# Step 2 of a sparse-attention graph layer: one block's sum moved in front of the mask, gathers issued one by one, a rearranged end

## The chip, the cores and the metric

The kernel runs on one core of one Trainium2 chip. The core has five engines that work at the same time, each through its own queue in order: the tensor engine (PE), the vector engine (DVE), the scalar engine (ACT), GpSimd (POOL), and SP, which here only issues DMA. The metric is device microseconds of one launch. The kernel before took 1431.23 us (median of 3 runs, 1426.26 to 1432.77).

## The reference

There are 3327 nodes with 256 features. `h = relu(layernorm(x))` goes through two diffusion steps along two paths:

```
Xf = R @ Xf                 # R: adjacency plus identity, rows divided by their sum (sparse: 0.12% filled)
A  = top-p attention of Xa  # softmax of q k^T, in each row only the largest entries that
                            # together reach 0.9 of the mass, divided by their sum
Xa = A @ Xa
Z  = Z + Xf @ U1[n].T + Xa @ U2[n].T      # n = 0, 1
out = x + layernorm(h + Z)
```

The attention is dense before it is cut: 3327 x 3327 exponentials per step, and a threshold per row. The threshold is what makes the kernel long; a row must be looked at several times until it is exact.

## The kernel before

Rows are worked on in 26 tiles of 128. For every tile the kernel does this:

- **weights** (L580): PE makes a row tile of logits in four pieces (`pl`, L598), ACT takes their exponential into `e`, 128 x 3328 (L602, L606).
- **measured** (`measured_twice` in step 2, L666): ACT passes three times over `e` and counts (`ja`, L631 in `through`), with short arithmetic of one value per row between the passes, on ACT, DVE and POOL. Out comes a guess that lies just above the threshold. POOL's part is L674 and L675, L687 to L689, and L694 to L709; the last of it, L709, feeds ACT's L711.
- **settle** (L722): DVE zeroes all that is above the guess and sums (L728), takes the largest 8 of every 168-wide segment (20 MAX8, L733), sorts some 48 candidates out of them (L740, L742), finds the exact threshold, and cuts `e` with it (L762, which this document calls the mask; L759, in two parts, for the first and last tile).
- **Sums** (L798): the cut `e` is transposed on PE block by block (`turn`, L811, 4 transposes of 128 x 128 into one of two PSUM banks `pt`), ACT copies each block to SBUF (`eT`, L813, three buffers), and PE multiplies it with the features (`sum`, L825, into the one PSUM bank `pa`). A tile has seven blocks, 0 to 6; block 6 is half as long.
- **spread**, **diffuse** (L1073, L908): the path of R. Five rows of the adjacency and of the features per node were gathered in step 1 by indirect DMA on POOL's queue; in step 2 the packed adjacency rows are loaded again by SP (L1094) and the features are gathered again (`fetched`, L899, five gathers of L903 per tile), and PE multiplies (`pr`, L911).
- **finish** (L934), only in step 2: DVE adds the two paths (L935, which frees `pa`), then comes the layer norm: DVE L457 and L458, POOL L464, L465, L943, ACT L950, POOL L945, L951 and L952, and the output.

No scheduler orders this. Each of these functions is a Python generator that emits a few instructions and then yields. The main loop (L1116) runs for every step over `i` = -1 to 27; in round `i` tile `i` is settled, tile `i+1` is measured, and the tile before is summed. A round has seven parts, `k` = 0 to 6, and the strings in `PLAN` (L1103) name by letter which generator goes on in which part: m measured, n the measured of the round before, d settle, c the settle of the round before, s spread, w weights, q their beginning, l the laws, g the gathers, f finish. `LAST` (L1106) replaces them for the last rounds. Whatever is left at the end of a round runs there (L1175). PE, ACT, DVE and, from step 2 on, POOL keep exactly this order of text (L1183), so an instruction that waits holds up everything written behind it on its engine.

In step 2 each part first transposes the block that lies two ahead of the one to be summed (L1160; `AHEAD`), then runs the letters, then sums one block (L1166). With `LATE[1] = 4` the parts 0 to 3 of round `i` sum blocks 3 to 6 of tile `i-2`, and parts 4 to 6 blocks 0 to 2 of tile `i-1`. The mask of tile `i-1` (letter c) is emitted in part 0 of round `i`, and the transpose of its block 0 in part 2, where the sum of block 5 of the tile before comes behind it.

`laws` (L548) computes for the tiles 3 to 25 the constants that `measured_twice` takes; its last piece is POOL arithmetic over 128 x 23 values (L567 to L574), emitted at the end of round -1 of step 2. `refetch(t)` (L1092) issues the load and all five gathers of a tile at once; round -1 issues those of tiles 0 and 1, round `i` those of tile `i+2`.

Of the kernel before, what the change touches and what calls it, by code (L numbers as in the profile page):

```python
# [9 lines left out]
F32 = mybir.dt.float32  # L10
# [3 lines left out]
AF = mybir.ActivationFunctionType  # L14
ALU = mybir.AluOpType
# [3 lines left out]
P = 128  # L19
N = 3327  # L20
D = 256
DA = 64
NT = (N + P - 1) // P
# [315 lines left out]
KT = DIRECT + 2  # L339
# [5 lines left out]
def guess_graph_layer(ctx, tc, x, adj, w1t, w2t, w3t, u1t, u2t, ln_g, ln_b, out, flag):  # L345
    nc = tc.nc

    const = ctx.enter_context(tc.tile_pool(name="const", bufs=1))
    nodes = ctx.enter_context(tc.tile_pool(name="nodes", bufs=1))
    scan = ctx.enter_context(tc.tile_pool(name="scan", bufs=1))  # L350
    adjp = ctx.enter_context(tc.tile_pool(name="adjp", bufs=3))
# [9 lines left out]
    V, G, S, PE = nc.vector, nc.gpsimd, nc.scalar, nc.tensor  # L361

    rows_of = lambda t: min(P, N - t * P)
    valid = lambda t: 0 <= t < NT
# [41 lines left out]
    half = const.tile([P, 4], F32, tag="half", name="half")  # L406
    for k, c in enumerate((-0.5, 0.5, -1.0, -0.5)):
        G.memset(half[:, k : k + 1], c)
    halves = const.tile([P, NT], F32, tag="halves", name="halves")
    G.memset(halves, 0.5)  # L410
    law = const.tile([P, 7, NT], F32, tag="law", name="law")
    one = const.tile([P, 7], F32, tag="one", name="one")
    for k, c in enumerate((1.0, -1.0, 5.0e-4, SQG[1], SQK[1], math.log(10.0), LNY)):
        G.memset(one[:, k : k + 1], c)
    of_s = const.tile([P, 4], F32, tag="of_s", name="of_s")
    for k, c in enumerate((SQG[0], SQG[2], -SQK[0], -SQK[2])):
# [24 lines left out]
    bx = dram.tile([P, NT, D + 1], F32, tag="bx", name="bx")  # L441
    vx = dram.tile([P, NT, D], F32, tag="vx", name="vx")
# [4 lines left out]
    bb = const.tile([P, TOPK + 1], F32, tag="bb", name="bb")  # L447
# [100 lines left out]
    def laws(ts):  # L548

        at = lambda k, a, b: law[:, k, a:b]  # L550
        few_of = [ts[h::2][n : n + 3] for n in range(0, len(ts), 3) for h in range(2)]
        for few in filter(len, few_of):
            pq = ps_t.tile([P, 4, P], F32, tag="pt", name="pq")
            pm = pq.rearrange("p a b -> p (a b)")[:, : 3 * (2 * DA + 2)].rearrange("p (t n) -> p t n", t=3)
            for k, t in enumerate(few):
                PE.matmul(pm[:, k, :], query_of(t), qm[query_at(t), 1, :], start=True, stop=True)
            wide = scan.tile([P, NP], F32, tag="w", name="wide")
            mq = wide[:, : 3 * (2 * DA + 2)].rearrange("p (t n) -> p t n", t=3)
            V.tensor_copy(mq[:, : len(few)], pm[:, : len(few)])
            V.tensor_copy(law[:, 2, few[0] : few[-1] + 1 : 2], mq[:, : len(few), DA])  # L560
            for k, t in enumerate(few):
                V.scalar_tensor_tensor(mq[:, k, : DA + 1], mq[:, k, : DA + 1], 1.0, mq[:, k, DA + 1 :],
                                       ALU.mult, ALU.mult, accum_out=at(1, t, t + 1))
            yield
        a, b = ts[0], ts[-1] + 1
        s, var, m = (at(k, a, b) for k in range(3))
        G.tensor_tensor(s, var, halves[:, a:b], ALU.pow)  # L567
        for k, c in ((3, SQG[0]), (4, SQG[2]), (5, -SQK[0]), (6, -SQK[2])):
            G.tensor_scalar(at(k, a, b), s, c, 1.0e-4, ALU.mult, ALU.add)
        G.tensor_tensor(at(4, a, b), at(4, a, b), var, ALU.add)  # L570
        G.tensor_tensor(at(4, a, b), at(4, a, b), m, ALU.add)
        G.tensor_scalar(m, m, 0.25, LNY - 0.25 * math.log(0.1 / N), ALU.mult, ALU.add)
        G.tensor_scalar(var, var, 0.125, None, ALU.mult)
        G.tensor_tensor(var, var, m, ALU.add)  # L574
# [51 lines left out]
    def con(k):  # L626
        return one[:, k : k + 1]
# [247 lines left out]
    def gathered(t):  # L875
        oh = ohs.pop(t)
        ls, n = lists[:, t, :], LIST - DIRECT
        po = ps_t.tile([P, 4, P], F32, tag="pt", name="po")
        PE.matmul(po[:, 0, : n + 1], oh, ls[:, DIRECT:], start=True, stop=True)
        lo = small.tile([P, n], F32, tag="lo", name="lo", bufs=2)  # L880
        S.copy(lo, po[:, 0, :n])
        nth = small.tile([P, 1], F32, tag="nth", name="nth")
        S.activation(nth, po[:, 0, n : n + 1], AF.Identity, scale=-1.0, bias=part)
        yield
        of = small.tile([P, LIST], F32, tag="of", name="of", bufs=2)
        V.scalar_tensor_tensor(of[:, :n], place[:, :n], nth, lo, ALU.is_equal, ALU.mult, accum_out=nth)
        G.tensor_scalar(index[:, t, DIRECT:], nth, -1.0, float(NONE), ALU.mult, ALU.add)
        ac = adjp.tile([P, KT, P], F32, tag="ac", name="ac", bufs=2)
        nc.sync.dma_start(ac[:, KT - 1, :], adj[t, :, t, :])
        acs[t] = ac  # L890
        G.tensor_tensor(ac[:, KT - 1, :], ac[:, KT - 1, :], ident, ALU.add)
        rows = adj.rearrange("t p j r -> (t p j) r")
        for k in range(KT - 1):
            G.indirect_dma_start(out=ac[:, k, :], out_offset=None, in_=rows,  # L894
                                 in_offset=bass.IndirectOffsetOnAxis(ap=index[:, t, k : k + 1], axis=0),
                                 element_offset=t * P * NT * P)
        xgs[t] = fetched(bx, t, D + 1)

    def fetched(table, t, w):  # L899
        xg = adjp.tile([P, KT - 1, D + 1], F32, tag="xg", name="xg", bufs=2)  # L900
        rows = table.rearrange("p j d -> (p j) d")
        for k in range(KT - 1):
            G.indirect_dma_start(out=xg[:, k, :w], out_offset=None, in_=rows,  # L903
                                 in_offset=bass.IndirectOffsetOnAxis(ap=index[:, t, k : k + 1], axis=0))
        return xg


    def diffuse(ac, xg, own, w):  # L908
# [94 lines left out]
    for q in range(HALF + 5):  # L1003
        if 0 <= q - 3 < HALF:
            k, pk = q - 3, made.pop(q - 3)
# [17 lines left out]
        if 0 <= q - 2 < HALF:  # L1023
            k, pt = q - 2, turned.pop(q - 2)
# [19 lines left out]
        if 0 <= q - 4 < HALF and 2 * (q - 4) in COUNTED:  # L1044
            k = q - 4
# [46 lines left out]
    def refetch(t):  # L1092
        acs[t] = adjp.tile([P, KT, P], F32, tag="ac", name="ac", bufs=2)
        nc.sync.dma_start(acs[t].rearrange("p k r -> p (k r)"), cx[t])  # L1094
        xgs[t] = fetched(vx, t, D)
        yield

# [1 line left out]


    PLAN = (("mdsssa", "mcdsssa", "edawwp", "msda", "mpdea", "gdwwq", "emgq"),  # L1103
            ("llcmss", "lnms", "lwwnfd", "lcmdsssg", "fmswqdf", "llmdf", "lmwfd"))

    LAST = {NT - 1: ("cfss", "cn", "ndd", "sss", "fddddsf", "f", "f"), NT: ("cf", "", "", "", "ff", "fv", "f"),  # L1106
            NT + 1: ("fv", "f", "", "", "f", "f", "f")}
    LATE = (1, 4)
    trace, begin = nc.cur_bb.bb.instructions, len(nc.cur_bb.bb.instructions)
    work = dict(m=none, d=none, f=none)  # L1110
    later = {}
    ordered = []
    for step in range(2):
        sums = Sums(step, live, xw if step else x0, AHEAD[step])

        for i in range(-1, NT + 2):  # L1116
# [4 lines left out]
            if step == 1 and i == -1:  # L1121
# [11 lines left out]
                e=first_end(i - 2) if step == 0 and valid(i - 2) else none,  # L1133
                a=itertools.islice(lister, 9 if i else 3) if step == 0 else none,
                p=packed(i + 1) if step == 0 and i >= 0 and valid(i + 1) else none,
                g=none if not valid(i + 2 * step) else refetch(i + 2) if step else gathered(i),
                b=none, q=none, v=proof() if step and i == NT else work.get("v", none),
                l=laws(range(3, NT)) if step and i == -1 else none,
            )
            if i >= 0 and valid(i + 3):  # L1140
                later[step, i + 3] = weights(step, i + 3, live)
# [9 lines left out]
                work["w"] = begun[2]  # L1151
            if step == 0 and i < 1:
                work["b"] = itertools.islice(product, MADE if i else NT)
            if step == 1 and i == -1:
                work["g"] = itertools.chain(refetch(0), refetch(1))
            for k in range(PARTS):
                g = PARTS * (i - 1) + k - LATE[step]
                summing = valid(g // PARTS)
                if summing and step:
                    sums.turn(g, min(i, NT - 1))  # L1160
                for c in "bb" + (LAST.get(i, PLAN[1]) if step else PLAN[0])[k]:
                    next(work[c], None)
                if summing and not step:
                    sums.turn(g, min(i, NT - 1))
                if summing:
                    ended = sums.sum(g)  # L1166
                    if ended and step == 0:
                        live["r", ended[0]] = ended[1]
                    elif ended:
                        work["f"] = finish(ended[0], live.pop(("f", ended[0])), *ended[1])  # L1170
            if step == 1 and i == -1:
                run(work["m"])
            if step == 0 and i == -1:
                G.memset(es[2][:, N:NP], 0.0)
            for c in "lcnwqsepgb" if step else "cmwqsepgb":  # L1175
                run(work[c])
            if step == 0 and i == NT:
                moments(1, gsum)
# [52 lines left out]
```

## Time and profile before

| | |
|---|---|
| median of 3 runs | 1431.23 us |
| profiled execution, its own time | 1383.37 us |
| its span | 1381.4 us |
| mean granted PE clock in it | 0.976 |
| PE busy | 1271.7 us, 92% |
| DVE busy | 1207.6 us, 87% |
| ACT busy | 1109.1 us, 80% |
| POOL busy | 1022.8 us, 74% |
| step 2 (from about 742 us) | some 640 us |

The profiled execution is shorter than the timed runs; its times can be compared with each other and with its own 1383.37. "Busy" counts instructions that an engine executes; waits between them are not in it. Ends of PE instructions are modelled, and spans on POOL are rough: a POOL instruction that is held up by another engine shows as a long one. In a line such as `[4.24 <-POOL g L674]` the engine stood idle for 4.24 us and was released by POOL's instruction of line 674. Matrix products in this data type are two passes, so four blocks of a sum appear as x8.

### The profile page before, as it was taken

The page shows a single profiled execution, that of the slowest core. Times are in us where ns is not written, and L with a number is a line of the kernel's source. Part 1 is how long each engine was busy: PE and PEld are TensorE (multiplying, and loading weights), DVE is VectorE, ACT ScalarE, POOL GpSimd, SP SyncE. Part 2 cuts the span into 40 slices and gives each one's busy share as a digit, 9 for nine tenths or more (in the row PEclk, how much of TensorE's full clock was granted, in tenths as well). Part 3 has the DMA queues.
Part 4 walks back from the last instruction along what each step waited for, and adds up shares of the span by engine and source line. Part 5 has one row for each costly group of instructions (what it writes and reads, how often), then busy time and mean ns, then how long its engine had stood idle before and what let it go on. Part 6 is the DMA issues. An engine that isn't in the chain of part 4 may idle for free.

```text
span 1381.4 us, 22149 instructions
## 1 busy us (share of the span) xinstructions
PE 1271.7 (92%) x6495; PEld 977.1 (71%) x6495; DVE 1207.6 (87%) x3595; ACT 1109.1 (80%) x2449; POOL 1022.8 (74%) x1374
## 2 busy tenths in 40 slices
PE   6898999999999999999997389999999999999885
PEld 5545777777877778787775267777776777777674
DVE  6878999999999999999944689999999999999992
ACT  5467888879888888888735689999999999999931
POOL 6225888888888888888843868888888888888832
PEclk9999999999999999999998589999999999999998
DMA  8884453545445453545331211212222221212100
GB/s 293 261 271 125 128 148 109 152 119 152 128 135 141 122 154 106 156 118 149 85 98 50 69 54 55 84 58 81 71 67 82 58 88 54 89 58 81 58 8 22
DMA packets 91202, 149.77 MB, mean 108 GB/s; under 512 B 15265, under 2 KB 58656, under 8 KB 91072
## 3 DMA queue, kind: packets, MB, share of 16 engines
q1 hardware_dynamic: 73616, 105.37, 24.4%
q0 software_dynamic: 16640, 42.69, 11.9%
q8 instruction: 54, 0.88, 0.3%
q14 instruction: 76, 0.62, 0.1%
q10 hardware_dynamic: 816, 0.20, 0.1%
HBM read 120.93 MB, written 27.28 MB: 107 GB/s over the span
## 4 chain that ended last, share of the span: by engine, by line
DVE 40%; PE 24%; ACT 17%; POOL 9%; DMA 4%; issue 4%; SPq 0%; POOLq 0%; DVEq 0%; ACTq 0%
ACT ja L631 11%; PE pa L825 9%; DVE e L762 9%; PE pl L598 5%; DVE cand L733 4%; DVE w L728 4%; DVE fm L847 4%; DVE bb L740 3%; DVE cand L742 3%; PE pt L811 3%; PE pz L988 3%; POOL xg L903 3%; POOL ac L894 2%; DVE x L762 2%; DMA at<-in_adj 2%
## 5 line engine op out<-in xcount | busy, mean ns | idle before, releaser
L825 PE MATMUL pa<-xw,eT 128*128 128x256 f32 x1352 | 330.8, 386 | 6.6 <-DVE s L935 6.5
L631 ACT ACTIVATE ja<-e,g 128x3328 uint8<-128x3328 f32 x106 | 325.8, 3074 | 0.1
L825 PE MATMUL pa<-x,eT 128*128 128x256 f32 x1352 | 323.1, 380 | 0.0
L825 PEld LDWEIGHTS pa<-xw,eT 128*128 128x128 f32 x1352 | 249.4, 191 | 67.9 <-issue 27.1
L825 PEld LDWEIGHTS pa<-x,eT 128*128 128x128 f32 x1352 | 243.7, 191 | 25.8
L733 DVE MAX8 cand<-w 128x8 f32<-128x168 f32 (+1 forms) x1040 | 251.5, 318 | 0.0
L813 ACT COPY eT<-pt 128x512 f32<-128x512 f32 (+1 forms) x364 | 201.9, 556 | 59.3 <-PE pt L811 58.8
L894 POOL DMA_INDIRECT ac<-in_adj,index x130 | 189.7, 1459 | 44.3 <-issue 30.5
L811 PE MATMUL pt<-ident,e 128*128 128x128 f32 x1144 | 180.1, 278 | 43.9 <-DVE e L762 21.9
L811 PEld LDWEIGHTS pt<-ident,e 128*128 128x128 f32 x1144 | 140.5, 144 | 90.2 <-issue 43.3
L903 POOL DMA_INDIRECT xg<-bx,index x130 | 158.0, 1216 | 39.2 <-issue 30.5
L728 DVE SCALAR_TENSOR_TENSOR w<-e,g 128x3328 f32<-128x3328 f32 x44 | 168.5, 3830 | 0.7
L903 POOL DMA_INDIRECT xg<-vx,index x130 | 130.9, 1007 | 45.6 <-issue 33.0
L762 DVE SCALAR_TENSOR_TENSOR e<-e,rec 128x3328 f32<-128x3328 f32 x40 | 153.6, 3840 | 0.6
L911 PE MATMUL pr<-xg,ac 128*128 128x257 f32 (+1 forms) x520 | 139.4, 392 | 11.3 <-DVE s L1086 11.1
L602 ACT ACTIVATE e<-pl 128x832 f32<-128x832 f32 x132 | 112.8, 859 | 30.2 <-PE pl L598 30.1
L911 PEld LDWEIGHTS pr<-xg,ac 128*128 128x128 f32 x520 | 94.0, 195 | 25.0 <-DVE s L1086 11.3
L740 DVE MAX8 bb<-cand 128x8 f32<-128x160 f32 x286 | 92.9, 325 | 6.4
L598 PE MATMUL pl<-after,qT 64*128 64x416 f32 x416 | 96.7, 559 | 0.6 <-ACT qT L527 0.6
L765 POOL TENSOR_TENSOR cum<-dr,bb 128x48 f32<-128x48 f32 x26 | 84.8, 3261 | 15.5 <-DVE rec L752 15.4
L951 POOL TENSOR_TENSOR s<-s,gam 128x256 f32<-128x256 f32 x25 | 92.6, 3703 | 3.2 <-ACT s L950 3.2
L598 PE MATMUL pl<-both,qT 64*128 64x416 f32 x416 | 90.1, 536 | 0.8 <-DVE both L1006 0.8
(257 smaller groups left out, 2200.0 us busy)
## 6 DMA issues: line engine op xcount, KB each, us to landing
at<-in_adj SPq DMA_DIRECT2D x102, 256.0 KB, 3.2
cx<-ac SPq DMA_DIRECT2D x26, 384.0 KB, 2.8
ac<-cx SPq DMA_DIRECT2D x26, 384.0 KB, 3.1
wide<-in_adj SPq DMA_DIRECT2D x10, 832.0 KB, 6.4
e<-in_adj SPq DMA_DIRECT2D x8, 832.0 KB, 5.1
bx<-e SPq DMA_DIRECT2D x26, 128.5 KB, 2.8
own<-bx SPq DMA_DIRECT2D x26, 128.5 KB, 3.2
x<-in_x SPq DMA_DIRECT2D x13, 256.0 KB, 5.4
```

The lines of the kernel that those rows point to most:

```text
L598: PE.matmul(pl[:, a, :wd], qT[p, :], keys_of(step, a).rearrange("p a b -> p (a b)")[:, c : c + wd], start=True, stop=True)
L631: S.activation(ja, e, f, bias=guess, scale=sign, accum_out=total)
L728: V.scalar_tensor_tensor(w, e, col(16), e, ALU.is_lt, ALU.mult, accum_out=d2)
L733: V.max(cand[:, 8 * s : 8 * s + 8], w[:, s * SEG : min(NP, (s + 1) * SEG)])
L740: V.max(b8, cand)
L762: V.scalar_tensor_tensor(e, e, at(1), e, ALU.is_ge, ALU.mult, accum_out=ra)
L811: PE.transpose(pt[:, j, :], e[:, (j0 + j) * P : (j0 + j + 1) * P], ident)
L813: S.copy(eT[:, :w, :], pt[:, :w, :])
L825: PE.matmul(self.pa, eT[:, c - 4 * k, :], self.xa[:, j, :], start=c == 0, stop=c == NT - 1)
L894: G.indirect_dma_start(out=ac[:, k, :], out_offset=None, in_=rows, in_offset=bass.IndirectOffsetOnAxis(ap=index[:, t, k : k + 1], axis=0), ...
L903: G.indirect_dma_start(out=xg[:, k, :w], out_offset=None, in_=rows, in_offset=bass.IndirectOffsetOnAxis(ap=index[:, t, k : k + 1], axis=0))
L911: PE.matmul(pr[:, :w], ac[:, k, :], own if k == KT - 1 else xg[:, k, :w], start=k == 0, stop=k == KT - 1)
```

## The change

- **The sum of block 5.** In step 2 part 1 sums blocks 4 and 5, and part 2 none (`BLOCKS`). Part 2 transposes blocks 0 and 1 of the next tile, one after the other (`g + (k == 2)`). On ACT both copies then stand in front of the two exponentials of that part. Transposes no longer wait for the first block that can be summed, so the first tile's come in the same pattern.
- **The gathers.** `fetched` yields after every gather, and one generator (`fetching`) goes through the tiles. `ggggg` in part 3 is one tile's five. For the rounds -1 to 3, `OPEN` spreads them otherwise: six in round -1, plus one at its end, four in round 0 plus one at its end, six each in rounds 1, 2 and 3, of which the sixth stands in part 5 between POOL's L689 and L694.
- **The laws.** What is left of them runs at the end of round 0 instead of round -1, and the square root by POOL (L567) becomes a logarithm and an exponential on ACT.
- **The end.** In round 25 DVE's L935 comes ahead of all twenty MAX8 (part 4, `fddddd`) instead of between the tenth and the eleventh. In round 26 the finish letters move from part 0 to parts 3 and 4, so that ACT's L950 comes behind the copies of the last tile's blocks 0 and 1.

SP's instructions keep their order. DVE's change in that one place.

```
@@ laws
-        G.tensor_tensor(s, var, halves[:, a:b], ALU.pow)
+        S.activation(s, var, AF.Ln, bias=con(7))
+        S.activation(s, s, AF.Exp, scale=0.5)
@@ gathered
-        xgs[t] = fetched(bx, t, D + 1)
+        run(fetched(bx, t, D + 1))
@@ fetched
-        xg = adjp.tile([P, KT - 1, D + 1], F32, tag="xg", name="xg", bufs=2)
+        xgs[t] = xg = adjp.tile([P, KT - 1, D + 1], F32, tag="xg", name="xg", bufs=2)
         for k in range(KT - 1):
...
-        return xg
+            yield
@@ refetch
-        xgs[t] = fetched(vx, t, D)
-        yield
+        yield from fetched(vx, t, D)
@@
...
-            ("llcmss", "lnms", "lwwnfd", "lcmdsssg", "fmswqdf", "llmdf", "lmwfd"))
-    LAST = {NT - 1: ("cfss", "cn", "ndd", "sss", "fddddsf", "f", "f"), NT: ("cf", "", "", "", "ff", "fv", "f"),
+            ("llcmss", "lnms", "lwwnfd", "lcmdsssggggg", "fmswqdf", "llmdf", "lmwfd"))
+    LAST = {NT - 1: ("cfss", "cn", "nd", "sss", "fdddddsf", "f", ""), NT: ("c", "", "", "ff", "ff", "fv", "f"),
             NT + 1: ("fv", "f", "", "", "f", "f", "f")}
+    OPEN = {-1: ("llcmss", "lnms", "lwwnfd", "lcmdsssggggg", "fmgswqdf", "llmdf", "lmwfdm"),
+            0: ("cmssggg", "nms", "wwnfd", "cmdsss", "fmgswqdf", "mdf", "mwfd"),
+            1: ("cmss", "nms", "wwnfd", "cmdsssggggg", "fmswqdf", "mgdf", "mwfd")}
+    OPEN[2] = OPEN[3] = OPEN[1]
+    fetching = itertools.chain(*(refetch(t) for t in range(NT)))
     LATE = (1, 4)
+    BLOCKS = ({}, {1: (0, 1), 2: ()})
@@ main loop
-                g=none if not valid(i + 2 * step) else refetch(i + 2) if step else gathered(i),
+                g=fetching if step else gathered(i) if valid(i) else none,
-                l=laws(range(3, NT)) if step and i == -1 else none,
+                l=laws(range(3, NT)) if step and i == -1 else work["l"] if step and i == 0 else none,
-            if step == 1 and i == -1:
-                work["g"] = itertools.chain(refetch(0), refetch(1))
-                if summing and step:
-                    sums.turn(g, min(i, NT - 1))
-                for c in "bb" + (LAST.get(i, PLAN[1]) if step else PLAN[0])[k]:
+                if step and valid((g + AHEAD[1]) // PARTS):
+                    sums.turn(g + (k == 2), min(i, NT - 1))
+                for c in "bb" + ({**OPEN, **LAST}.get(i, PLAN[1]) if step else PLAN[0])[k]:
                     next(work[c], None)
-                if summing:
-                    ended = sums.sum(g)
+                for n in BLOCKS[step].get(k, (0,)) if summing else ():
+                    ended = sums.sum(g + n)
+            if step and i < 1:
+                next(fetching)
-            for c in "lcnwqsepgb" if step else "cmwqsepgb":
+            for c in ("lcnwqsepb" if i > -1 else "cnwqsepb") if step else "cmwqsepgb":
                 run(work[c])
```

The constant 0.5 for the power (a memset of 128 x 26) goes, and one more constant column is set.

More of the change, by code (lines that the diff above doesn't have):

```diff
@@ L408, in guess_graph_layer @@
         G.memset(half[:, k : k + 1], c)
-    halves = const.tile([P, NT], F32, tag="halves", name="halves")
-    G.memset(halves, 0.5)
     law = const.tile([P, 7, NT], F32, tag="law", name="law")
-    one = const.tile([P, 7], F32, tag="one", name="one")
-    for k, c in enumerate((1.0, -1.0, 5.0e-4, SQG[1], SQK[1], math.log(10.0), LNY)):
+    one = const.tile([P, 8], F32, tag="one", name="one")
+    for k, c in enumerate((1.0, -1.0, 5.0e-4, SQG[1], SQK[1], math.log(10.0), LNY, 1.0e-12)):
         G.memset(one[:, k : k + 1], c)
```

## The prediction

> **What bounds the kernel now.** I read the busy shares first, then the same by stage, then the chain of waits inside step 2, then the waits of each engine, and last the timelines of the two ends of step 2. The stages (columns: window, its length, busy us of PE, PE loads, DVE, ACT, POOL, then PE clock, DMA share, GB/s):
>
> ```profile
> 742.00:811.50 69.50, 38.47 (x162) 26.77 (x162) 46.66 (x180) 52.26 (x104) 45.34 (x72) 0.68 0.21 59
> 811.50:1322.40 510.90, 481.42 (x2472) 374.36 (x2471) 475.09 (x1335) 479.99 (x955) 427.55 (x568) 1.00 0.23 69
> 1322.40:1381.40 59.00, 36.82 (x186) 30.65 (x184) 29.53 (x81) 9.16 (x18) 15.31 (x21) 0.90 0.06 18
> ```
>
> The change leaves step 1 alone, so only these 640 us matter. In the middle row PE, DVE and ACT are each 93 to 94% busy: no engine alone is the bound, a loop through all three is. Mask starts (L762) lie 22.2 us apart. One turn of the chain of waits (start, length, what):
>
> ```profile
> 944.39 4.12 DVE e L762 x2
> 948.51 0.14 issue
> 948.65 0.63 PE pt L811 x4
> 949.28 1.60 PE pl L598 x8
> 950.88 1.92 PE pa L825 x8
> 952.80 0.45 PE pt L811 x4
> 953.27 0.58 ACT eT L813
> 953.86 3.07 ACT ja L631 x2
> 956.93 0.02 issue
> 956.95 0.23 DVE g L682
> ```
>
> The mask ends; PE transposes block 0, makes logits, sums the old tile's block 5 (the 1.92), transposes block 1; ACT copies that and only then counts (ja); DVE waits for the count. The sum of block 5 needs nothing of the new mask, yet it stands on this path. The waits of that stretch (total us, times, longest) price it:
>
> ```profile
> PE pt L811 <- DVE e L762: 16.6, 14, 1.5
> DVE g L682 <- ACT ja L631: 10.9, 22, 0.9
> ACT eT L813 <- PE pt L811: 10.6, 20, 0.6
> DVE g L696 <- ACT ja L631: 4.9, 21, 0.2
> ```
>
> Per turn: PE idles 1.16 us for the mask, ACT 0.54 for block 1, DVE 0.48 and 0.23 for counts. What is to be won is about half a microsecond a turn, not 1.92. Opening and end, from ACT's, POOL's and PE's timelines (start, length, instruction, idle before and its releaser):
>
> ```profile
> 777.57 0.29 ACT L685 ACTIVATE g<-g 128x1 f32<-128x1 f32 x1 [4.24 <-POOL g L674]
> 784.17 0.27 POOL L687 TENSOR_SCALAR g<-g 128x1 f32<-128x1 f32 x1
> 1335.58 3.44 PE L825 MATMUL pa<-xw,eT 128*128 128x256 f32 x8 [3.14 <-DVE s L935]
> 1350.58 0.66 PE L811 MATMUL pt<-ident,e 128*128 128x128 f32 x4 [3.12 <-ACT eT L813]
> ```
>
> In the opening two small POOL operations stand behind ten gathers and the laws; at the end PE waits for a DVE sum queued behind ten MAX8, and then for copies queued behind ACT's L950.
>
> **What the Trainium skill says.** "SBUF — State Buffer", section "Who interferes with whom": a DVE instruction with two SBUF inputs and a GpSimd instruction that reads SBUF exclude each other for a whole instruction. The trace agrees and shows its price: POOL's L951 takes 4.1 us beside a mask and 0.73 without, and once L708, normally 0.30, took 3.70 beside the mask at 1033.28; the next mask came after 23.06 us. The same section only infers that descriptor writing is spared by such DVE instructions; here the first gather beside L728 took 4.54 us against 0.95. "Perfetto Trace Analysis", section on the tensor engine's instruction, calls ACT, DVE and GPSIMD strict FIFO: that is the wait behind L950 above. "TensorE: Matmul & The Clock Gate", Part 1: an idle PE falls to half clock; the sum after 3.14 us of idling took 3.44 against 1.99. "ScalarE: Activation LUTs", section "Table sets: the hidden batching unit": Ln and Exp share a set, so the new pair should load no table; ACT already alternates them.
>
> **Part 1, block 5 in front of the mask, blocks 0 and 1 behind it (23 turns).** Nothing is added or removed; on PE one sum of 4 blocks moves up and one transpose group follows its neighbour, on ACT the copy of block 1 goes ahead of two exponentials (L602). No DMA moves. Times below count from mask end, 948.50.
> ACT: the first count ends at 1.98 as now. Block 0 and 1 copied (0.46 + 0.48), two exponentials (2 x 0.85), second count and its read 3.16: done at 7.78 instead of 8.4. The 0.54 wait is gone.
> DVE: it has 7.97 us of work up to L682 (L935 ends at 956.47), so DVE, not ACT, now ends that wait.
> The loop is then 7.97, plus 0.50 (L682 to L684, 956.95 to 957.45), plus 5.64 (L684 to the third count's end, 963.09), plus 0.11 to L696, plus 7.52 (L696 to the next mask's end, 970.72) = 21.74. ACT's own loop is 22.22 - 0.60 = 21.62, below it. Gain 0.48 a turn.
> PE: L935 reads the only pa bank, so the next sum cannot start before 8.02. From there through blocks 0 to 5 is 14.40 (956.88 to 969.55, plus 1.73). PE reaches the transposes at 22.42, that is 0.68 after the mask's end at 21.74 instead of 0.14. Both transposes and two logit pairs take 2.7, done at 3.4; ACT wants the last at 3.77. Spare 0.35. The stall moves from the mask to L935 (about 0.9), where it costs nothing. PSUM banks: block 1 takes that of block 6, copied 1.2 before mask end.
> POOL: from L728's end its queue brings L694 at 14.25 and L709 at 17.25; the mask starts at 17.64. It slips through with 0.4 to spare (0.45 now).
>
> **Part 2, gathers one by one.** The 130 gathers stay, each 0.95 to 1.1 plus 0.30 of issue. Now L674 of tile 1 stands behind L567 to L574 (763.61 to 770.5) and five gathers (to 777.2), and L687 behind five more. Afterwards one gather comes before L694, one after L709, then L674 at 766.1 (ready when L673 ends), three gathers, and L687 as soon as L686 is done. So ACT's L685 runs at 773.4, not 777.57; the third count ends at 777.1; DVE's L696 starts at 778.1, when its MAX8 are through, not 784.48: 6.4 us.
> The two new ACT operations on 128 x 23 cost about 0.65 (two dependent ones, from L619 and L620) in ACT's queue; the POOL pow goes, whose 4.04 is mostly lock beside L728. The law arithmetic, 2.8 us, now falls behind mask 0 and L728 and delays L765 and so DVE's L769 to about 792.5; the wait of 2.4 there eats part of the room, but L696 of the next tile still comes at 801.65 against 808.09. Gain to mask 1: 6.4.
> Against it: three turns get a gather between L689 and L694 (1.25). POOL has 0.53 spare, so L709 comes about 0.4 too late and is locked out by the mask; as at 1033.28 that delays L711 by 1.4, of which ACT has 0.2 to spare. Price 1.2 each. Relative to now those three turns lose 1.1, 0.75, 0.75 = 2.6. SP's queue keeps its order; its loads wait on the same readers.
>
> **Part 3, the end.** L935 of tile 23 goes ahead of twenty MAX8: 1333.2 instead of 1335.52, 2.3 earlier for PE. With PE idle nearly as long before it, I keep the slow first sum. PE then ends block 5 of tile 24 at 1346.7, transposes two blocks of tile 25 (their part of the mask ends at 1344.6), ends block 6 at 1348.5, and with L935 the last tile's sum starts at about 1349.2 instead of 1354.84. L950 no longer stands ahead of those copies. From there on 13.4 us as now, then the same tail. Gain 5.6.
> The memset dropped and the constant added at the start are hidden under the input loads (0.1 if not).
>
> **Sum.** 6.4 - 2.6 + 20 x 0.48 (9.6) + 5.6 = 19.0. The profiled execution's own time, 1383.37, becomes 1364. The runs' median, 1431.23, is 47.9 above that execution; nothing on the page says where those lie, so I carry them over: 1412.
>
> **Rivals.**
> PE slower in the runs than in this profile. The 48 us would fit a PE some 7% slower, for step 1 is 98% PE. Then the turn is PE's own: the loop from L935 through sums, transposes, logits and the second count is 4.1 + 17.1 x 1.07 = 22.4, against 17.6 + 4.6 x 1.07 = 22.5 now. Part 1 gives 2, the total is 11: 1420. Against: the clock shown is 1.00 here.
> No lockout in the opening, law arithmetic fast, PE warm at the end: L696 two earlier, 2.6 not lost, 1.5 at the end, 6 more: 1406. For: POOL spans are rough.
> The change does part of what it says: L935 becomes the gate, 0.68 grows past 1.03 and the turn stays near 22.1; only both ends gain: about 10, 1421; if POOL's lock also takes the opening, 4 and no measurable change. For: the spare times are 0.35 and 0.4.
> Slower: the mask locks POOL out in every second turn. Place: L708/L709 against L762. If a gather or L765 runs 0.4 us longer than here, as one gather did by 1.7 before 1033, such turns take 23.0 to 23.1. Every second turn gives an average of 22.4, 0.2 x 20 = 4 lost; every turn 0.8 x 20 = 16, against 9 won at the ends: +7, 1438. It decides from about 11 locked turns in 20 for no gain over all, from about 19 for slower by 0.5%. Against: DVE alone cannot start the mask before 17.5, and L709 starts at 17.25; a locked turn gives POOL back its spare time.
>
> **Chances.** Forecast 0.47, slower PE 0.20, no lockout 0.10, ends only 0.10, no change 0.06, lockout 0.07. I call 0.5% (7 us) the bound of what the three runs, 6.5 apart, can tell from no change. Faster: the first and third, and five sixths of the two that end near 1420, close to the bound at 1424: 0.82; same, with the other sixth: 0.11; slower 0.07. The range goes from the no-lockout case with a turn of 21.4 (1398) to the edge of no change (1428).
>
> **What would show it.** Turns of 21.7 us in the middle; no wait of eT on block 1 and of PE on L762; instead PE pa waiting on L935 about 0.9 a turn; L682 without a wait. L696 of tile 1 at about 778, mask 1 at about 805. The last pa sum ending 19 us earlier with 13.4 us after the last L935 wait. L709 of 3.7 us in three turns only; more of them, or turns at 22.2, and the forecast is wrong in part 1; L674 still behind gathers, and it is wrong in part 2.

## The result and the profile after

| | before | after |
|---|---|---|
| median of 4 runs each | 1429.2 us (1426.26 to 1432.77) | 1405.72 us (1404.97 to 1409.1) |
| ratio | | 0.9838, 95% interval 0.9816 to 0.9859 |
| profiled execution, its own time | 1383.37 us | 1406.04 us |
| its span | 1381.4 us | 1404.0 us |
| step 1, mask to mask | 23.86 us | 25.45 us |
| step 2, first exponential to the end | 637.5 us | 617.3 us |

The change makes the kernel 1.6% faster. The two profiled spans say the opposite, 1404.0 against 1381.4, and must not be set against each other: step 1, which the change doesn't touch, took 25.45 us a turn in one and 23.86 in the other (the first experiment comes back to it). So each time below counts from the first exponential of step 2, ACT's L606 before, L605 after. In the profile after, the lines named here have numbers one or two lower: the mask is L761, the last sum L934, POOL's last law L708.

| us from the first exponential of step 2 | before | after | gain on this stretch |
|---|---|---|---|
| to mask 0 | 44.00 | 37.51 | 6.49 |
| mask 0 to mask 1 | 23.61 | 21.82 | 1.79 |
| mask 1 to mask 4 | 66.26 | 67.14 | -0.88 |
| mask 4 to mask 23 (19 turns) | 422.81 | 414.08 | 8.73 |
| mask 23 to mask 24 | 21.81 | 23.44 | -1.63 |
| mask 24 to the end | 59.01 | 53.27 | 5.74 |
| sum | 637.5 | 617.3 | 20.24 |

The stages of step 2 after, in the same view by stretch as before (window, its length, busy us of PE, PE loads, DVE, ACT, POOL, then PE clock, DMA share, GB/s):

```profile
784.80:846.10 61.30, 36.17 (x171) 26.49 (x170) 46.74 (x181) 52.55 (x106) 39.85 (x69) 0.75 0.22 63
846.10:1350.70 504.60, 480.56 (x2464) 378.39 (x2463) 473.60 (x1334) 479.47 (x955) 432.28 (x571) 0.99 0.24 70
1350.70:1404.00 53.30, 35.38 (x186) 29.71 (x184) 30.14 (x81) 9.11 (x18) 15.44 (x21) 0.91 0.07 20
```

All three rows are shorter: 69.5 to 61.3, 510.9 to 504.6, 59.0 to 53.3. Hardly any work is gone; ACT is busy for 52.3 us at the opening before and for 52.6 after. What went is idle time. One turn in the chain of waits after (start, length, what):

```profile
1000.32 4.13 DVE e L761 x2
...
1009.67 2.35 DVE cand L732 x10
1012.02 0.38 DVE s L934
...
1012.81 0.40 ACT g L683
...
1015.51 3.07 ACT ja L630 x2
1018.68 0.28 DVE g L695
```

Before, the chain left the mask for PE and the counts of ACT; now it stays on DVE, through ten MAX8 and L934, and goes to ACT only for the third count. The waits of the middle stretch (total us, times, longest):

```profile
PE pa L824 <- DVE s L934: 22.1, 21, 3.7
DVE g L695 <- POOL nm L942: 6.3, 18, 0.4
ACT eT L812 <- PE pt L810: 4.0, 3, 2.7
ACT g L683 <- DVE g L682: 3.4, 10, 1.8
```

PE's wait for the mask is gone from the list and one for L934 stands there instead; ACT's 20 small waits for block 1 are gone (what is left is 3, one of them 2.7), and DVE's wait for the second count has gone from 22 times to 2, 0.7 us in all. The second line names POOL's L942, but L695 reads nothing of it: in the chain above the third count ends at 1018.58 and L695 starts 0.1 us later. The opening, the long turn, round 24 and the end, from the timelines of ACT, POOL and PE (start, length, instruction, idle before and its releaser):

```profile
816.27 0.29 ACT L684 ACTIVATE g<-g 128x1 f32<-128x1 f32 x1
889.30 3.48 POOL L707 TENSOR_SCALAR g<-g 128x1 f32<-128x1 f32 x1
1339.43 3.65 PE L824 MATMUL pa<-xw,eT 128*128 128x256 f32 x8 [3.75 <-DVE s L934]
1377.39 1.99 PE L824 MATMUL pa<-xw,eT 128*128 128x256 f32 x8 [1.12 <-DVE s L934]
```

The first line answers ACT's L685 before, whose 4.24 us of idling for POOL are gone. The second is the POOL law of one value per row, otherwise 0.3 us, held beside the mask at 888.92; this turn took 24.29 us. The third is round 24, where no logits are left to make: PE stood for 3.75 us and this turn took 23.44. The fourth is the last wait for L934; the last sum of `pa` ends 13.4 us behind it.

### The profile page after: what moved, and what is told of

It reads as the page before. It is cut to its first block, busy times and chain, and to the rows that moved or that the text cites. A ratio compares the mean times of both kernels' runs of the same rounds, so it can differ in the third digit from the quotient of the medians.

```text
span 1404.0 us, 22150 instructions
## 1 busy us (share of the span) xinstructions
PE 1277.2 (91%) x6495; PEld 978.9 (70%) x6495; DVE 1197.7 (85%) x3595; ACT 1106.7 (79%) x2451; POOL 953.8 (68%) x1373
## 3 DMA queue, kind: packets, MB, share of 16 engines
q1 hardware_dynamic: 73616, 105.37, 23.9%
## 4 chain that ended last, share of the span: by engine, by line
PE 43%; ACT 24%; DVE 20%; POOL 7%; issue 4%; DMA 1%; another core or an unknown queue 0%; SPq 0%; ACTq 0%; DVEq 0%; POOLq 0%
PE pa L824 18%; ACT ja L630 9%; PE pt L810 6%; PE pr L910 4%; DVE w L727 4%; PE pl L597 4%; DVE cand L732 4%; ACT eT L812 4%; PE pz L987 3%; PE pz L923 3%; DVE e L761 2%; DVE x L761 2%; POOL xg L902 1%; ACT e L601 1%; DVE bb L739 1%
## 5 line engine op out<-in xcount | busy, mean ns | idle before, releaser
L824 PE MATMUL pa<-xw,eT 128*128 128x256 f32 x1352 | 325.2, 385 | 27.5 <-DVE s L934 25.7
L810 PE MATMUL pt<-ident,e 128*128 128x128 f32 x1144 | 176.6, 277 | 14.9 <-DVE e L758 6.7
L902 POOL DMA_INDIRECT xg<-bx,index x130 | 152.9, 1176 | 44.2 <-issue 31.9
L893 POOL DMA_INDIRECT ac<-in_adj,index x130 | 130.2, 1001 | 44.6 <-issue 30.5
L761 DVE SCALAR_TENSOR_TENSOR e<-e,rec 128x3328 f32<-128x3328 f32 x40 | 153.0, 3825 | 0.6
L927 POOL TENSOR_TENSOR sv<-sv,x 128x256 f32<-128x256 f32 x26 | 20.1, 775 | 110.2 <-ACT sv L926 110.2
L764 POOL TENSOR_TENSOR cum<-dr,bb 128x48 f32<-128x48 f32 x26 | 82.6, 3176 | 15.4 <-DVE rec L751 15.4
```

The costliest lines, as they stand in the source:

```text
L761: V.scalar_tensor_tensor(e, e, at(1), e, ALU.is_ge, ALU.mult, accum_out=ra)
L810: PE.transpose(pt[:, j, :], e[:, (j0 + j) * P : (j0 + j + 1) * P], ident)
L824: PE.matmul(self.pa, eT[:, c - 4 * k, :], self.xa[:, j, :], start=c == 0, stop=c == NT - 1)
```

## The experiments

### The kernel before again

No edit.

> The kernel before once more, nothing changed. In its first profile a turn of step 1 lasts about 24.0 us and the execution 1383 us, in that of the changed kernel 25.5 us, though the change touches nothing in step 1. If that execution was a single quick one, this profile shows 25 to 25.5 us a turn in step 1 and about 1425 to 1432 us in all. If the change made step 1 slower, it shows 24.0 again. Step 2 has mask intervals of 22.2 us in either case. Timed against before: ratio 1.000.

Measured: 1426.82 us, ratio 0.9994 (0.9981 to 1.0007). In its profile step 1 takes 25.43 us a turn, and step 2 takes 637.37 us from its first exponential, against 637.5 in the first profile of this kernel. This profile's own time is 42.2 us above the first one's, and its step 2 starts 42.3 us later, at 786.23 instead of 743.90. So nearly all of what separates the first profile from the timed runs lies ahead of step 2, and step 2 can be compared between any two profiles. It does not come from the kernel: the runs below were made on three chips, and on one of them (for the runs e5 to e8) this kernel's median was 1387.64 us, on the other two 1427.44 and 1427.73. Each chip served for one group of runs, so chip and time of day are not told apart.

### One part at a time

Each from the kernel before. Part 1:

```
+    BLOCKS = ({}, {1: (0, 1), 2: ()})
-                if summing and step:
-                    sums.turn(g, min(i, NT - 1))
+                if step and valid((g + AHEAD[1]) // PARTS):
+                    sums.turn(g + (k == 2), min(i, NT - 1))
-                if summing:
-                    ended = sums.sum(g)
+                for n in BLOCKS[step].get(k, (0,)) if summing else ():
+                    ended = sums.sum(g + n)
```

> Only part 1: block 5 summed in front of the mask, blocks 0 and 1 transposed behind it. Forecast's theory: mask intervals of 21.74 to 21.79 us instead of 22.2 in the middle of step 2, some 20 of them, 9 to 10 us less, with PE waiting for L935 about 1 us a turn; about 1420 us. Rival (L935 becomes the gate and nothing is won): intervals stay at 22.1 to 22.2 and the time within 3 us of before. Rival (lockout by the mask in every second turn): intervals alternate between 21.8 and 23, and the time is the same or longer.

Part 2, with all of the change's lines on gathers and laws, of which these are the core:

```
-            ("llcmss", "lnms", "lwwnfd", "lcmdsssg", "fmswqdf", "llmdf", "lmwfd"))
+            ("llcmss", "lnms", "lwwnfd", "lcmdsssggggg", "fmswqdf", "llmdf", "lmwfd"))
+    OPEN = {-1: ("llcmss", "lnms", "lwwnfd", "lcmdsssggggg", "fmgswqdf", "llmdf", "lmwfdm"),
+            0: ("cmssggg", "nms", "wwnfd", "cmdsss", "fmgswqdf", "mdf", "mwfd"),
+            1: ("cmss", "nms", "wwnfd", "cmdsssggggg", "fmswqdf", "mgdf", "mwfd")}
```

> Only part 2: gathers one by one and laws moved, sums and end as before. Forecast's theory: the masks of tiles 0 and 1 come about 6.4 us earlier than before, counted from the first exponential of step 2; a part of that is lost again where the sixth gather of rounds 1 to 3 makes POOL late, so 4 to 6 us less in all; about 1424 us. Rival (gathers and laws were hidden anyway): mask 0 where it was, time the same.

Part 3:

```
-    LAST = {NT - 1: ("cfss", "cn", "ndd", "sss", "fddddsf", "f", "f"), NT: ("cf", "", "", "", "ff", "fv", "f"),
+    LAST = {NT - 1: ("cfss", "cn", "nd", "sss", "fdddddsf", "f", ""), NT: ("c", "", "", "ff", "ff", "fv", "f"),
```

> Only part 3: the end's order. Forecast's theory: nothing changes up to mask 24, then 59.0 us to the end become about 53.4, 5.6 less; about 1424 us. Rival (the tail of the last layer norm and PE's work bound it anyway): 59 us as before.

Measured, with step 2 from each profile, against 637.4 in the kernel before on that chip:

| | ratio (interval) | step 2, us | gain | where |
|---|---|---|---|---|
| part 1 | 0.9929 (0.9911 to 0.9947) | 627.04 | 10.3 | turns of 21.79; mask 0 to mask 1 takes 20.72, not 23.55; the turn before mask 24 and the end lose 1.1 and 1.6 |
| part 2 | 0.9957 (0.9943 to 0.9971) | 631.02 | 6.4 | 6.48 up to mask 0; turns of 22.2 |
| part 3 | 0.9970 (0.9954 to 0.9986) | 631.76 | 5.6 | 5.7 behind mask 24, nothing ahead of it |

Each part gains where it was priced to gain. Part 1's 10.3 us are 10.2 between masks 1 and 23, 2.8 ahead of them and a loss of 2.7 behind them; the last two had no price. Inside part 2 the gathers and the laws were not tried apart, nor inside part 3 L935 and L950, so how much each of them brings is not shown. The three gains make 22.3 us, the whole change 20.1. The turn between masks 3 and 4 explains most of it: it takes 21.81 with part 1 alone and 22.66 with part 2 alone, but 24.29 with both.

### The long turn: gathers caught up earlier

```
-    OPEN = {-1: ("llcmss", "lnms", "lwwnfd", "lcmdsssggggg", "fmgswqdf", "llmdf", "lmwfdm"),
-            0: ("cmssggg", "nms", "wwnfd", "cmdsss", "fmgswqdf", "mdf", "mwfd"),
-            1: ("cmss", "nms", "wwnfd", "cmdsssggggg", "fmswqdf", "mgdf", "mwfd")}
+    OPEN = {-1: ("llcmss", "lnms", "lwwnfd", "lcmdsssggggggg", "fmgswqdf", "llmdf", "lmwfdm"),
+            0: ("cmss", "nms", "wwnfd", "cmdsssgggg", "fmgswqdf", "mdf", "mwfd"),
+            1: ("cmss", "nms", "wwnfd", "cmdsssggggg", "fmswqdf", "mdf", "mwfd")}
```

> The changed kernel, with the gathers of the first rounds put elsewhere: nine ahead of the first mask and six in the round after it, so that rounds 1 to 3 have five gathers and no sixth. Theory (the 24.29 us turn between the masks of tiles 3 and 4 is POOL's law arithmetic held for 3.5 us beside a mask, because a sixth gather made it late): that turn falls to about 21.8, the two before it stay 21.1 to 21.8, and 2.5 us are gone from the first exponential of step 2 to the end (617.3 to about 614.8; ratio to the kernel before about 0.982). Rival (the long turn comes from the count in tile 4 or from the wait for L934 alone, and not from the gathers): a turn above 23 remains in the same place, and nothing is gained.

Measured: the turn between masks 3 and 4 takes 21.78, step 2 takes 614.84, 2.4 less than in the changed kernel; ratio to before 0.9831 (0.9812 to 0.985). The same POOL instruction in this kernel's timeline, ahead of the mask of tile 3 at 853.77:

```profile
852.95 0.33 POOL L707 TENSOR_SCALAR g<-g 128x1 f32<-128x1 f32 x1
```

It comes 0.8 us ahead of that mask and takes 0.33 us, not 3.48. Without the sixth gather there is no lock and no long turn. But the lock by itself doesn't make 24.29. The run below with only the sum moved has it too, 3.48 us in the same place, and its turn takes 23.10. The two differ in PE's sum behind the lock, first in the changed kernel, then in that run:

```profile
901.90 3.24 PE L824 MATMUL pa<-xw,eT 128*128 128x256 f32 x8 [1.67 <-DVE s L934]
899.91 1.99 PE L824 MATMUL pa<-xw,eT 128*128 128x256 f32 x8 [1.74 <-DVE s L934]
```

So of the 2.5 us above an ordinary turn about 1.3 are the lock, and about 1.2 a sum that ran slowly after PE had waited; the granted PE clock was 0.58 from 902 to 905 in the changed kernel, and 1.00 from 900 to 903 in the other run.

### What sets the turn: eight and twelve MAX8 ahead of L682

```
-            if s in (NSEG // 2 - 1, NSEG - 1):
+            if s in (NSEG // 2 - 1 - 2 * step, NSEG - 1):      # eight
+            if s in (NSEG // 2 - 1 + 2 * step, NSEG - 1):      # twelve
```

> The changed kernel, with 8 instead of 10 MAX8 of step 2 ahead of the first sum of three counts (L682) in VectorE's order, 12 instead of 10 behind it; nothing else moves. Theory (the stretch on VectorE from the end of the mask over the last block's sum and ten MAX8 to L682, 7.97 us, sets the turn): the sum comes about 0.5 us earlier, the turn falls from 21.8 to about 21.65 where ScalarE's or TensorE's own work sets it, about 3 us less over the step. Rival 1 (TensorE's transposes and sums already set the turn): 21.78 as before. Rival 2 (the second half of the MAX8 and what follows, now longer, holds the mask): longer, by up to 0.5 us a turn, 10 us in all.

> The changed kernel with 12 instead of 10 MAX8 of step 2 ahead of L682 and 8 behind it. With 8 ahead the turn fell only from 21.79 to 21.73. Theory (VectorE's stretch from the mask's end to L682 sets the turn of the changed kernel, and ScalarE's loop of 21.73 lies close under it): L682 comes 0.48 later and the turn grows by as much, to about 22.27, 10 us over the step (617.3 to about 627). Rival (ScalarE's, POOL's or TensorE's loop sets it, and VectorE has room): 21.8, unchanged.

Measured with twelve: turns of 22.26, that is 0.47 longer, and two MAX8 take 0.47 (ten take 2.35 in the chain above); step 2 takes 626.4, the ratio is 0.9933 (0.991 to 0.9956). In the chain of waits DVE goes from the mask to L682 without a gap, with the MAX8 now as

```profile
1011.21 2.82 DVE cand L732 x12
1014.03 0.38 DVE s L934
```

Measured with eight: turns of 21.73, 0.06 shorter, step 2 616.25, ratio 0.983 (0.981 to 0.9849). Its chain of waits no longer goes by the mask:

```profile
1005.78 3.05 ACT ja L630 x2
1008.83 0.95 ACT eT L812 x2
1009.78 1.70 ACT e L601 x4
1011.48 3.06 ACT ja L630 x2
...
1014.56 0.22 DVE g L681
```

Both counts, both copies and the exponentials follow each other on ACT without idling. So DVE's stretch sets the turn of the changed kernel, microsecond for microsecond where it is longer, and ACT's own loop lies only 0.06 below it. The expected 21.65 was 0.08 too low, and so 3 us was too much to hope for. An earlier mask also has a price: with eight, POOL's L708 is held for 3.59 us beside the mask of tile 1 and L707 for 3.56 beside that of tile 3, and the turns from there take 22.79 and 23.19.

### What PE's waits for L934 cost: the last sum behind three MAX8

```
-            if s in (NSEG // 2 - 1, NSEG - 1):
+            if s in ((2, 9, NSEG - 1) if step else (NSEG // 2 - 1, NSEG - 1)):
...
-            ("llcmss", "lnms", "lwwnfd", "lcmdsssggggg", "fmswqdf", "llmdf", "lmwfd"))
+            ("llcmss", "lnms", "lwwnfd", "lcmdsssggggg", "fdmswqdf", "llmdf", "lmwfd"))
```

`OPEN` and `LAST` get the same `d`.

> The changed kernel, with the last block's sum (L934) behind three MAX8 in each turn of step 2 instead of ahead of all of them; the number of MAX8 ahead of L682 stays, so that L682 comes as late as before. This puts L934's end 1.2 to 1.5 us later and tells what TensorE's 21 waits for it cost. Written as the other way round than the waits: theory A (the waits for L934 cost nothing in the ordinary turn, since L682 sets it): turn 21.8 as in the changed kernel, TensorE's waits longer by 1.2 us a turn. Theory B (the wait for L934 sets the turn, TensorE being without slack behind it): 1.2 us more in each turn, 24 us in all. In the turn without logits (23.44 us) both give a longer one.

The expectation has the direction of the edit wrong. In the changed kernel L934 stands behind ten MAX8, as the chain above shows, so behind three it comes 1.6 us earlier, not later. What tells the two theories apart holds with the sign turned: A says turns of 21.8 all the same, B says shorter ones. Measured: 21.79 in the ordinary turn. PE's stall goes back to the mask; the waits of PE between 950 and 1300:

```profile
PE pt L810 <- DVE e L761: 7.4, 10, 0.7
PE pt L810 <- DVE x L761: 3.9, 6, 0.7
```

So theory A holds: the waits for L934 were slack in the ordinary turn, and where PE takes its rest doesn't matter there. In round 24 it does: its turn takes 21.81, not 23.44. Both theories had a longer turn there for a later L934, so a shorter one for an earlier L934 fits both. There PE has no logits to make and arrives early, and ACT waits for its blocks. Step 2 takes 613.9, 3.4 less than in the changed kernel: 1.6 in round 24, 1.2 in the turn between masks 3 and 4 (23.07; L707 is still held, for 3.42, so these 1.2 are the slow sum that is missing here), the rest over other turns. Ratio 0.9828 (0.9804 to 0.9851).

### Which half of part 1 counts

The changed kernel, once with only the sum moved, once with only the two transposes in a row:

```
-                    sums.turn(g + (k == 2), min(i, NT - 1))
+                    sums.turn(g, min(i, NT - 1))               # sum moved only
-    BLOCKS = ({}, {1: (0, 1), 2: ()})
+    BLOCKS = ({}, {})                                          # two transposes only
```

> The changed kernel with one half of part 1 undone: the second last block's sum stays in front of the mask, but block 1 is transposed where it was, behind block 0's logits. Theory (ScalarE's wait for block 1 came from the 1.92 us sum that stood between; without it block 1 comes as soon as the logits, and the loop through VectorE's 7.9 us sets the turn as in the changed kernel): turns of 21.8. Rival (the two transposes in a row are what saves the time): turns of 22.0 to 22.2, and ScalarE's wait for block 1 is there again, 0.3 to 0.5 us a turn.

> The changed kernel with the other half of part 1 undone: blocks 0 and 1 are transposed in a row behind the mask, and the second last block's sum follows the logits, as before. Theory (block 1 comes early either way, and TensorE, idle for 1.16 us in a turn of the kernel before, has room for the sum behind the mask): turns of 21.8, TensorE waiting for the mask and not for L934. Rival (moving the sum is what saves the time, since otherwise the last sums come later and L934 with them): turns of 22.0 to 22.2.

Measured with the sum alone: turns of 21.75 to 21.91 in the middle, step 2 616.58, ratio 0.9875 (0.9848 to 0.9903). ACT's wait for block 1 is not in its list of waits between 950 and 1300. That is nearly all of part 1's gain in the ordinary turn, 21.82 on average against 21.79 with both halves and 22.21 before; that step 2 is even shorter than in the changed kernel comes from the turn behind mask 3 (23.10) and from round 24 (22.91). Measured with the transposes alone: turns of 23.9 to 25.6, step 2 674.69, ratio 1.0193 (1.017 to 1.0217), slower than the kernel before. Neither theory had that. The waits of ACT between 950 and 1300, and one of them in ACT's timeline:

```profile
ACT eT L812 <- PE pa L824: 41.1, 15, 3.9
```

```profile
1005.69 0.59 ACT L812 COPY eT<-pt 128x512 f32<-128x512 f32 x1 [2.20 <-PE pa L824]
```

ACT's copy of block 1 waits for a sum, not for a transpose. `eT` has three buffers; blocks 5, 6 and 0 hold them, and block 1 can be copied only when the sum of block 5 has read its own. That sum stands behind the mask here, at 1003.66, and ends at 1005.65; ACT, and both counts behind the copy, wait for it. With the sum in front of the mask a buffer is free in time. In the kernel before, ACT's copy waited for block 1's transposes, which stand behind the same sum on PE.

### How near the lockout is: 0.6 us more on POOL

```
+        G.tensor_tensor(nm, rstd, half[:, 1:2], ALU.pow)
         G.tensor_scalar(nm, mv[:, 0:1], rstd, -1.0, ALU.mult, ALU.mult)
```

The added operation's result is overwritten by the next line.

> The changed kernel with one more small power operation of about 0.6 us in POOL's queue in each turn from the first L942 on (its result is overwritten's input, without effect). Theory of the rival that had the kernel slower (POOL reaches L707 only 0.4 us ahead of the mask; 0.6 more and the mask locks it out for 3.5 us): many turns of 23 to 24.3 in place of 21.79, every second one at least, 12 to 25 us more over the step. Rival (POOL has more room than that, or catches up): turns of 21.8 to 21.9, under 3 us more.

Measured: turns of 22.66 and 21.93 in alternation, step 2 627.13, 9.9 us more than in the changed kernel; ratio 0.9937 (0.9913 to 0.9961). POOL's and ACT's timelines at one long turn, the mask at 1023.67:

```profile
1023.94 3.60 POOL L708 TENSOR_SCALAR g<-g 128x1 f32<-128x1 f32 x1
1027.57 0.30 ACT L710 ACTIVATE g<-g 128x1 f32<-128x1 f32 x1 [0.95 <-POOL g L708]
```

Twelve such locks of L707 or L708 are in the trace, against one in the changed kernel. A locked turn lasts 0.7 longer than its neighbour, POOL has that much more time, and in the next turn nothing is held. The expected number of locks came, every second turn, but the 9.9 us stay under the 12 to 25 expected, because the price of a lock was set too high (turns of 23 to 24.3).

### Three edits together

The changed kernel with the gathers caught up, eight MAX8 ahead of L682 and L934 behind three of them.

> Three edits together on the changed kernel: the gathers caught up before the first mask (as in the run with nine and six), 8 instead of 10 MAX8 ahead of L682, and L934 behind three of them. If each is worth by itself what its theory says (2.5 us for the locked turn, 3 us for the turn), and L934's place costs nothing, about 5.5 us less than the changed kernel from the first exponential of step 2 to the end (about 612), 1400 us or a ratio of about 0.980. If L934's place matters, the turn is longer than 21.8.

Measured: 1360.28 us where the kernel before takes 1387.64 on that chip, ratio 0.9805 (0.9787 to 0.9822). Turns of 21.70 to 21.74 from mask 2 to mask 24, no L707 or L708 held by a mask, step 2 612.06: 5.2 us less than in the changed kernel. Its timed ratio lies 0.3% under those of the three runs above that hold one of its edits each (0.9831, 0.983, 0.9828), where the intervals overlap; the gain of 5.2 us rests on the traces.

## Why the prediction came out as it did

**The sum.** 19.0 us were predicted for step 2, and 20.24 are measured. That they lie so close is partly luck. The opening (6.4, measured 6.49) and the end (5.6, measured 5.74) came as priced. The turns between masks 1 and 23 gave 7.85 where 7.0 were predicted (9.6 less 2.6), with a smaller gain and a smaller loss inside. The two turns without a price, +1.79 and -1.63, nearly cancel. Of the 6.3 us between the predicted 1412 and 1405.72, 2.0 come from the starting median, which went from 1431.23 with three runs to 1429.2 with four, and 1.2 from step 2. The other 3 can't be placed; the runs of before lie 6.5 apart.

**The carried 47.9 us.** To carry them over was right, and the rival that read them as a slow PE in step 2 named the wrong thing: the kernel before, run again, is 42.3 us later at the start of step 2, and its turn there is unchanged. The rival's 1420 would have needed turns that shrink by 0.1.

**Part 1, the turn.** Predicted 21.74, measured 21.79. The terms, with the mask's end at 1004.43: 7.89 to L681 (7.97 predicted), 0.49 to L683 (0.50), 5.77 to the third count's end (5.64), 0.10 to L695 (0.11), 7.54 to the next mask's end (7.52). Twelve MAX8 show that this is the loop that sets the turn. PE reached the transposes 0.65 after the mask's end (0.68) and waited 0.83 for L934 (0.9), at no cost. The ordinary turn gained 0.42, not 0.48: 8.73 us came between masks 4 and 23, but 1.14 of them from one turn, the one that the prediction names as locked (23.06 before, 21.92 after, and 21.93 with part 1 alone). One term was too low: ACT's own loop, 21.62 in the prediction, is 21.73 by the run with eight MAX8, so that the room under the turn was 0.06 and not 0.12. It didn't matter here. And the reasoning behind "the 0.54 wait is gone" was incomplete: it counted the PSUM banks and not the three `eT` buffers. The sum's move alone gives nearly all of the gain; the two transposes in a row add 0.03 a turn to it, and without the move step 2 is 57 us longer than with it.

**Part 1, two turns it did not price.** The first turn, mask 0 to mask 1, got 1.8 us shorter where nothing was predicted: the forecast had L695 of the next tile 57.75 us behind the first exponential and it came at 55.90. Part 1 alone takes 2.8 off this turn. Round 24, without logits, got 1.6 longer: the step "the stall moves to L935, where it costs nothing" fails where PE has nothing else to do in that time. L934 behind three MAX8 gives the 1.6 back. How slowly PE's first sum runs there counts too: with part 1 alone, and with only the sum moved, it took 2.7 and 2.6 us instead of 3.65, and the turn 22.9 instead of 23.4.

**Part 2.** Predicted 6.4 to mask 0, measured 6.49. ACT's L684 came 29.53 us behind the first exponential and DVE's L695 34.09 (29.5 and 34.2 predicted). L768 waited 1.0 and not 2.4 for POOL's L764. The two new operations on ACT took 0.52 (0.65 predicted), with no idle time before either. The three lockouts at 1.2 each became one turn that is 2.5 too long: masks 1 and 2 were not reached, and at mask 3 the lock cost about 1.3 against a price of 1.2, as the runs without the slow sum show (23.10 and 23.07), and the sum of 3.24 behind PE's wait of 1.67 cost as much again. The net of -2.6 over these three turns was measured as -0.88, with turns of 21.11 and 21.74 ahead of the long one. The cause and the price stood as predicted, the number of times did not, and the slow sum was not foreseen. It is what "SBUF — State Buffer", section "Who interferes with whom", in the Trainium skill describes, and the trace agrees: L707, on one value per row, took 3.48 us beside a mask that takes 3.69.

**Part 3.** Predicted 5.6, measured 5.74 in the change and 5.7 alone, with the predicted 13.4 us from the last wait for L934 to the end of the last sum. Inside, the slow first sum that I kept did not come in round 25: PE had idled for 2.53 us and took 1.99. It came in round 24, 3.65 after 3.75 us. That a PE that has idled runs slower for a while is what "TensorE: Matmul & The Clock Gate", Part 1, states, and the trace agrees there. But the length of the idling alone doesn't decide: behind mask 3 the sum took 3.24 after 1.67 of idling, and in round 25, after the same 2.52 to 2.53, it took 1.99 in five profiles, 2.40, 3.48 and 3.68 in three others. So the part of the forecast that kept it was a guess; behind mask 24 it is worth a few tenths either way (53.3 us with 1.99, 53.4 with 3.48, 53.6 with 3.68).

**The rivals.** "No lockout" has the number that came, 1406, but not by its reasons. Some of its terms came: L695 was 1.85 us earlier, and 1.7 of the 2.6 were not lost. But it needs 25 us in step 2, and 20.24 were measured: there was a lockout, and the warm PE in round 25 was worth a few tenths and not 1.5. The rest of the way to 1406 is the lower median and the 3 us that can't be placed. "Ends only" is refuted by the turn. "Slower by lockouts" has its mechanism confirmed by the added POOL operation: about every second turn is locked, with a mean turn of 22.3 where the rival said 22.4. Its sum holds too: with half of the turns locked the kernel still beats the one before. Its example was misread: ahead of 1033 in the kernel before, no gather ran 1.7 longer; POOL stood idle for 1.73 ahead of a gather that took 1.11. Locks in every turn were never reached: the turn behind a locked one had none.

## What to carry to other kernels

Before an instruction is moved ahead, list what it frees as well as what it waits for: here the sum stood between the mask and block 1, on PE in the old order and through the copy buffer in the new one, so its move paid by itself, and its companion, the early transposes, was harmful without it. A stall that is moved to where it "costs nothing" costs in the rounds at the end, where the work that covers it is missing; price those rounds by themselves. When the same loop runs through several engines, test the stretch that seems to set it by adding a little and taking a little away: two MAX8 more cost all of their 0.47 us, two fewer gave 0.06, and that shows both what sets the turn and the room under it. And a total that comes as predicted proves little until its terms are set side by side: two unpriced terms cancelled here.

## What was not expected of the hardware

The same kernel takes 1387.64 us on one chip and 1427.44 and 1427.73 on two others. The profiles of the runs made there place the difference in step 1, with turns of 23.9 to 24.2 us on the first chip and of 25.4 to 25.6 on the others. In the first profile of the kernel before, POOL's gathers of the adjacency took longer than in the second, 1459 ns on average against 1001, so it is not shorter gather instructions that make step 1 short. Both profiles have the same instructions in the same order on every engine. In the long one PE stands 1.3 us a turn for a copy of ACT (L522 for L813, 30.2 us in 23 waits), which the short one doesn't have. Why stays open; step 2 agrees within 0.2 us.

A sum of eight matmuls that PE starts after 1.7 to 2.6 us of idling takes 1.99 us in one execution and over 3 in another, in kernels that differ little. It is worth up to 1.2 us where that sum lies on the path, and what decides it is not shown here.
